# Four edits to a two-block ConvNeXt-style kernel: who asks for x1's rows, when blocks are stored, how many tile reads per place, and how the first pass gives memory back

## The chip, the cores and the metric

The kernel runs on one core of a Trainium2 chip, in one launch. The metric is device time in microseconds, the median of several runs. The engines are TensorE (PE, with its weight loads shown as PEld), VectorE (DVE), ScalarE (ACT), GpSimd (POOL) and SyncE (SP), which only issues DMAs. POOL and ACT can issue DMAs too. Each engine executes its own instructions in order.

## The reference

The input x has shape (8, 96, 96, 192), and all of it is float32. There are two residual blocks, each behind a GroupNorm `gn` with 32 groups. Cut to what matters here:

```python
proj  = einsum('bhwd,dc->bhwc', gn(x), W_in) + b_in          # 192 -> 384 channels
local = depthwise 3x3 convolution of proj
mixed = 0.25 * (four running averages of local: left, right, down, up) + local
x1    = x + layernorm(mixed) @ W_out + b_out                  # 384 -> 192

y = depthwise 7x7 convolution of gn(x1) + dw_bias
y = layernorm(y) * ln_gamma + ln_beta
h = gelu(y @ w0 + b0)                                         # 192 -> 768
out = x1 + (h @ w1 + b1) * gamma                              # 768 -> 192
```

## The kernel before, in words

The work runs in stages. The trace shows them in this order.

The **first pass** (to about 753 us) normalises x, transposes it, multiplies by W_in and writes the projection to a DRAM tensor `P_d`. The last tile is stored by `store_a` (L410 and below), in parts for its channel thirds (`whole(m, eng)`) and one for an edge row.

The **second pass** (770 to 1795 us) loads projection channels (`pin`, issued at L613) and a band of convolution weights (L608), computes the 3x3 convolution as matmuls with banded weights (L626), and does the running averages as scans on DVE (L659, L668) and matmuls. The **third** (to about 2628 us) applies the layer norm and W_out, and writes x1 to DRAM as `X` (`X1_d` in the code).

Then the **7x7 convolution** is done in 32 steps n, one for each half of the batch and each group of channels. A step n loads three raw pieces of x1's rows (`load_raw(n, t)`, t = 0, 1, 2, two DMAs of 384 KB each, L839), loads a band of weights (`load_band`, L849) that DVE copies to the other partitions (`spread`, L877), scales the raw pieces into `xin` (L871 on ACT for the steps in question), runs six convolutions (`conv_d`, 24 matmuls per channel pair, L1196), has ACT write the result into `yo` (L1206), and stores it to DRAM as `Y` with six DMAs on SP (`store_d`, L1222, L1226, L1227).

The **last stage** computes layer norm, both dense layers and the output. It loops over u = 0..72; two values of u share one tile of `Y`, read as two buffers `ya` and `yb`, each in 20 pieces (`load_y`, 60 KB pieces at L1255 and 16 KB pieces at L1261). A tile also needs `r`, the rows of x1 it is added to: `load_r` (L1276, 1536 KB) and `bias_r`, an addition on POOL (L1282). In each u, DVE sums, centres and scales the rows (`norm_steps_e`: L1338, L1331, L1359, and so on), POOL computes the power -1/2 of the variance (L1365), DVE spreads that (L1321 to L1324) and transposes (L1386), PE does the first dense layer (`first_layer`, L1401 and L1411), ACT the gelu (L1420), and PE the second dense layer of the u before (`second_layer`, L1431), after which DVE adds r (L1442) and POOL stores the output (L1450).

The convolutions n = 0..18 run before this loop, and n = 19..31 (`N1` is 19) are laid into it. The order of all of this is written by hand inside `tc.manual_schedule()`. A loop over u calls `slot()` five times; from u = 2 on, each call takes one entry of the list `slots`. A step n has nine entries: three with a third of the scales each, then six with a convolution each. So step n's nine entries spread over nearly two loops u. Besides that, each `slot()` call issues seven steps of the list `loads`, the reads of the next-but-one tile of `Y` (41 steps, begun once per two u).

In the kernel before, the first entry of a step n also asks for its own third raw piece, since only two buffers hold the raw pieces of an inlaid step; the entries after that ask for the first two pieces of n + 1. All are asked for by SP. The last entry, behind the last convolution, asks for the six stores of n and for the band of n + 1. SP's queue in these loops therefore holds the tile's reads ya and yb, r between them, the raw pieces, the stores and the bands, in the order in which the code emits them.

Waits between engines are placed by the framework from the order of emission and from tile lifetimes. Tile pools are opened and closed per stage; a pool opened with `reuse_waits="tile"` lets a later tile on the same memory wait only for the earlier tiles that lay there. Every DMA on the queues of SP and ACT signals its landing on one of eight semaphores, taken in turn, and POOL's DMAs have eight of their own.

Of the kernel before, what the change touches and what calls it, by code (L numbers as in the profile page):

```python
# [101 lines left out]
def conv_blocks_kernel(  # L102
# [40 lines left out]
    L = 2 * S - 1  # L143
    GS = D // GROUPS

    const = ctx.enter_context(tc.tile_pool(name="const", bufs=1))
    dram = ctx.enter_context(tc.tile_pool(name="dram", bufs=1, space=DRAM))

# [2 lines left out]
    RB = 32  # L151
# [50 lines left out]
    SQ = 1.0 - DECAY * DECAY  # L202
    KAPPA = 1.0 / (0.25 * GAIN * SQ)
    ab_pool = ExitStack()
    mp = ab_pool.enter_context(tc.tile_pool(name="ab_const", bufs=1))
    mix = mp.tile([128, NJ, 128], F32, name="mix")
    zero = mp.tile([128, GB, S], F32, name="zero")
    nc.gpsimd.memset(zero, 0.0)
# [27 lines left out]
        (slice(0, 128), 2, slice(DH, D)),  # L236
    )
    with ExitStack() as ph:
        cp = ph.enter_context(tc.tile_pool(name="a_const", bufs=1))
        xp = ph.enter_context(tc.tile_pool(name="a_x", bufs=6))  # L240
        sp = ph.enter_context(tc.tile_pool(name="a_small", bufs=2))
        tp = ph.enter_context(tc.tile_pool(name="a_t", bufs=2))
        op = ph.enter_context(tc.tile_pool(name="a_out", bufs=2))
        zp = ph.enter_context(tc.tile_pool(name="zprep", bufs=1))
        ps_t = ph.enter_context(tc.tile_pool(name="a_ps_t", bufs=2, space=PSUM))
        ps_m = ph.enter_context(tc.tile_pool(name="a_ps_m", bufs=2 * NC, space=PSUM))

        avg = cp.tile([S, 128], F32, name="avg")
        nc.vector.memset(avg, 1.0 / S)
        win = cp.tile([128, 3, C], F32, name="win")  # L250
        for p, k, c in spans:
            nc.scalar.dma_start(win[p, k], W_in[c])
        bin_ = cp.tile([128, NC], F32, name="bin_")
        with nc.allow_non_contiguous_dma(reason="one bias per partition"):
            nc.scalar.dma_start(bin_, b_in.rearrange("(m p) -> p m", p=128))

# [155 lines left out]
        def store_a(po, b, k):  # L412
            at, g = b % GB, b // GB
            final = b == B - 1 and k == NK - 1

            def whole(m, eng):
                eng.dma_start(
                    P_d[
                        g, m * 128 : (m + 1) * 128, k * WA : (k + 1) * WA, at
                    ].rearrange("p r j h -> p r (j h)"),  # L420
                    po[:, m].rearrange("p r j h -> p r (j h)"),
                )

            whole(0, nc.gpsimd)
            if not final:
                for m in range(1, NC):
                    whole(m, nc.gpsimd)

            for edge, r, row, js in (
                (NK - 1, WA - 1, RB, (0, NJ - 1)),  # L430
                (0, 0, RB + 1, (1, NJ)),
            ):
                if k == edge:
                    to = slice(1 - js[0], NJ - js[0])
                    (nc.sync if final else nc.gpsimd).dma_start(
                        P_d[g, :, row, at, to].rearrange("(m p) j h -> p m (j h)", p=128),
                        po[:, :, r, js[0] : js[1]].rearrange("p m j h -> p m (j h)"),
                    )
            if final:
                for m in range(1, NC):  # L440
                    whole(m, (nc.sync, nc.gpsimd)[m % 2])

        def zero_edge(i):

# [53 lines left out]
        with tc.manual_schedule():  # L498
            for n in range(NK):
                for j in range(NJ):  # L500
                    load_a(n, j)
            for n in range(NK, 6):
                for j in range(NJ):
                    load_a(n, j)
            load_kernels()
            bn, last, cols = stats_a(0)
            for step in bn + last:
                step()
            xT = tp.tile([128, 3, WA // 2, S], F32, tag="xT", name="xT")
            for k in range(3):  # L510
                turn(0, cols, xT, k)
            for b in range(B):
                more = b + 1 < B
                for t in range(n_t):
                    u = b * n_t + t

                    n, j = divmod(u - 2, NJ)
                    if j == 0 and n + 6 < n_x:
                        for j in range(NJ):
                            load_a(n + 6, j)  # L520
                    if t == 0 and more:
                        bn, last, nxt_cols = stats_a(b + 1)
                    if u in rest:
                        rest[u]()

                    def ahead(n):
                        if more:
                            for _ in range(n):
                                bn.pop(0)()

                    def end(i):
                        if more:
                            for _ in range(ends.get((t, i), 0)):
                                last.pop(0)()

                    cur = xT
                    if t + 1 < n_t or more:
                        to = cols if t + 1 < n_t else nxt_cols
                        xT = tp.tile([128, 3, WA // 2, S], F32, tag="xT", name="xT")
                        turn_next = lambda k: turn(u + 1, to, xT, k)  # L540
                    else:
                        turn_next = lambda k: None
                    k, j = divmod(t, NJ)
                    if j == 0:
                        po = op.tile([128, NC, WA, NJ, S], F32, tag="po", name="po")
                    pms = project_full(cur)
                    end(0)
                    ahead(share[t] // 2)
                    turn_next(0)
                    turn_next(2)  # L550
                    project_rest(cur, pms, po, j)
                    end(1)
                    ahead(share[t] - share[t] // 2)
                    turn_next(1)
                    if j == NJ - 1:
                        store_a(po, b, k)
                if more:
                    cols = nxt_cols

# [8 lines left out]


    NI = len(place)  # L570
    by_tile = dict(reuse_waits="tile")
    gn_pool = ExitStack()
    gp = gn_pool.enter_context(tc.tile_pool(name="gn", bufs=1, side="right", **by_tile))
    pre = gp.tile([128, 2 * GS, ZW], F32, tag="band", name="c_pre")
# [13 lines left out]
    with ExitStack() as ph:  # L588
# [10 lines left out]
        nc.vector.memset(decay[:, :, 0:1], 0.0)  # L599
        decay_f = decay.rearrange("p b h -> p (b h)")  # L600

        def load_b(k):
            c = slice(k * CC, (k + 1) * CC)
            band = bp_.tile([128, CC, 3, RB], F32, tag="band", name=f"band0_{k}")
            pin = bp_.tile([128, CC, GB, NJ, S], F32, tag="pin", name=f"pin_{k}")
            for g in range(NG):
                p = g * 64
                nc.sync.dma_start(  # L608
                    band[p : p + RB + 4].rearrange("p c t o -> p (c t o)"),
                    ZB_d[:, c].rearrange("r c t o -> r (c t o)"),  # L610
                )
                for lo, hi in ((0, RB), (RB, RB + 1), (RB + 1, RB + 2)):
                    nc.sync.dma_start(  # L613
                        pin[p + lo : p + hi].rearrange("p c b j h -> p c (b j h)"),
                        P_d[g, c, lo:hi].rearrange("c r b j h -> r c (b j h)"),
                    )
            return band, pin

        def conv_b(band, pin, i, last):
            pls = [ps_l.tile([128, GB, S], F32, tag="pl", name="pl") for _ in range(NG)]  # L620
# [69 lines left out]

        n_k = C // CC
        with tc.manual_schedule():
            loads = [load_b(k) for k in range(3)]
            locs, lasts, zs, mos, todo = {}, {}, {}, {}, []

            def add(k, i):
# [115 lines left out]
    s1 = early.tile([128, 2, NH, 2, GROUPS], F32, name="s1")  # L812
    todo = [(hf, i) for hf in range(2) for i in range(NI)]
    N1 = NI + 3
    d_pools = [early, None]
    raws, bands, xins, yos = {}, {}, {}, {}

    def load_raw(n, t):

        hf, i = todo[n]  # L820
        if n >= N1 or ((n == 0 or n % 2) and t < NT - 1):
            pool, bufs = early, NT - 1
        elif n == 0 or n % 2:
            pool, bufs = gp, 1
# [4 lines left out]
        row = NGC * NV * GC * WQ  # L829
        run = NV * GC * WQ  # L830
        x1 = X1_d[hf]
        engs = (nc.sync, nc.gpsimd) if n < 2 else (nc.gpsimd,) * 2 if n < N1 else (nc.sync,) * 2
        for g, eng in enumerate(engs):
            src = bass.AP(
                tensor=x1.tensor,
# [619 lines left out]
    with tc.manual_schedule():  # L1455
# [55 lines left out]
                load_raw(N1, t)  # L1511
        gn_pool.close()
        yp = ctx.enter_context(tc.tile_pool(name="e_yT", bufs=2, side="right", **by_tile))
        rp = ctx.enter_context(tc.tile_pool(name="e_r", bufs=2, side="right", **by_tile))
        tp = ctx.enter_context(tc.tile_pool(name="e_t", bufs=2, side="right", **by_tile))

        slots = []
        for n in range(N1, len(todo)):
            more = n + 1 < len(todo)
            scales = scale_steps(n)  # L1520
            per_t = len(scales) // NT
            slots += [scales[:per_t], scales[per_t : 2 * per_t], scales[2 * per_t :]]
            slots[-3].append(lambda n=n: load_raw(n, NT - 1))
            if more:
                for t in range(NT - 1):
                    slots[t - 2].append(lambda n=n, t=t: load_raw(n + 1, t))
            slots += [[lambda n=n, c=c: conv_d(n, c, ps_y)] for c in range(GS)]
            slots[-1].append(lambda n=n: store_d(n))
            if more:
                slots[-1].append(lambda n=n: load_band(n + 1))  # L1530

        loads = []

        def slot():

            if slots and u >= 2:
                for step in slots.pop(0):
                    step()
            for step in loads[:7]:
                step()  # L1540
            del loads[:7]

        load_r(0, nc.gpsimd)
        for k in range(3):
# [94 lines left out]
```

## Time and profile before

| | |
|---|---|
| median of 3 runs | 5538.36 us (5535.46 to 5547.05) |
| the profiled execution's own time | 5532.09 us |
| its span, first to last instruction | 5530.3 us |
| granted TensorE clock, mean | 0.981 |
| PE busy | 5295.1 us (96%) |
| DVE, ACT, POOL busy | 3600.3, 2587.0, 2317.4 us |

Times in the profile are microseconds from the start of the span. A line of a timeline gives the start, the length, the engine, the line of the kernel, the operation, and the tiles written and read; in square brackets stands how long the engine was idle before it and what ended that. "SPq", "POOLq" and "ACTq" are the DMA requests that an engine's queue makes, with the time that making them took. In lists of waits, the columns are the total, the number of times and the longest, all for a pair of "who waited" and "for what". Matmuls of 32-bit data appear as several records, so counts of matmuls in the profile are larger than in the code.

### The profile page before, as it was taken

The page shows a single profiled execution, that of the slowest core. Times are in us where ns is not written, and L with a number is a line of the kernel's source. Part 1 is how long each engine was busy: PE and PEld are TensorE (multiplying, and loading weights), DVE is VectorE, ACT ScalarE, POOL GpSimd, SP SyncE. Part 2 cuts the span into 40 slices and gives each one's busy share as a digit, 9 for nine tenths or more (in the row PEclk, how much of TensorE's full clock was granted, in tenths as well). Part 3 has the DMA queues.
Part 4 walks back from the last instruction along what each step waited for, and adds up shares of the span by engine and source line. Part 5 has one row for each costly group of instructions (what it writes and reads, how often), then busy time and mean ns, then how long its engine had stood idle before and what let it go on. Part 6 is the DMA issues. An engine that isn't in the chain of part 4 may idle for free. (4 is left out here: it accounts for less than half of the span.)

```text
span 5530.3 us, 108052 instructions
## 1 busy us (share of the span) xinstructions
PE 5295.1 (96%) x42206; PEld 3366.3 (61%) x42206; DVE 3600.3 (65%) x6722; ACT 2587.0 (47%) x5778; POOL 2317.4 (42%) x2021
## 2 busy tenths in 40 slices
PE   6999989999999999999788999999999999999999
PEld 4666643333333899899445555666566667767767
DVE  6656449999999455555556555555467777667764
ACT  2444447777777566565435444444433332332332
POOL 1111128888888455555322222222233333333332
PEclk9999989999999999999899999999999999999999
DMA  7999879999997899899996555555433233333331
GB/s 224 286 289 268 237 195 244 246 241 247 243 245 209 256 291 290 266 286 300 294 281 164 119 121 127 125 134 131 111 91 82 80 80 78 83 94 83 80 79 40
DMA packets 793774, 1015.27 MB, mean 184 GB/s; under 512 B 330623, under 2 KB 669696, under 8 KB 791216
## 3 DMA queue, kind: packets, MB, share of 16 engines
q1 hardware_dynamic: 700104, 673.23, 47.8%
q0 software_dynamic: 82976, 331.44, 18.4%
q8 instruction: 333, 5.46, 0.4%
q10 hardware_dynamic: 10184, 3.70, 0.3%
q14 instruction: 177, 1.45, 0.1%
HBM read 603.70 MB, written 419.95 MB: 185 GB/s over the span
## 5 line engine op out<-in xcount | busy, mean ns | idle before, releaser
L1431 PEld LDWEIGHTS hp<-w1g,g 128*128 128x128 f32 x6912 | 1118.6, 190 | 141.4 <-issue 74.0
L1431 PE MATMUL hp<-w1g,g 128*128 128x192 f32 x6912 | 1175.6, 329 | 0.0
L1420 ACT ACTIVATE g<-hp,b0g 128x512 f32<-128x512 f32 x864 | 518.3, 690 | 1149.9 <-PE hp L1411 1149.8
L1450 POOL DMA_DIRECT2D out_dram<-xo x288 | 210.5, 731 | 1647.9 <-DVE xo L1442 1554.0
L1401 PE MATMUL hp<-yT,w0w 128*128 128x512 f32 x1728 | 781.1, 598 | 10.8 <-DVE yT L1386 10.8
L1442 DVE TENSOR_TENSOR xo<-hp,r 128x384 f32<-128x384 f32 x288 | 227.5, 790 | 816.4 <-PE hp L1431 812.1
L1032 PE MATMUL po<-wc,mt 128*128 128x193 f32 x3456 | 688.0, 335 | 9.1 <-DVE x1c L1049 9.1
L626 PE MATMUL pl<-pin,band 34*32 34x380 f32 (+1 forms) x13824 | 628.7, 490 | 20.4 <-DMA pin<-P_d 20.4
L700 POOL TENSOR_TENSOR mo<-mo,z 128x768 f32<-128x768 f32 x286 | 597.2, 2088 | 4.4 <-ACT mo L651 0.4
L1032 PEld LDWEIGHTS po<-wc,mt 128*128 128x128 f32 x3456 | 557.3, 192 | 40.5 <-ACT mean L1034 30.2
L1196 PE MATMUL hp<-xin,band 63*64 63x372 f32 (+1 forms) x4608 | 433.4, 510 | 126.7 <-ACT yo L1206 39.6
L1401 PEld LDWEIGHTS hp<-yT,w0w 128*128 128x128 f32 x1728 | 322.5, 191 | 373.5 <-issue 337.8
L659 DVE TENSOR_TENSOR_SCAN z<-decay,loc 128x768 f32<-128x768 f32 x288 | 505.8, 1756 | 46.0 <-ACT loc L635 16.5
L668 DVE TENSOR_TENSOR_SCAN z<-decay,z 128x768 f32<-128x768 f32 x288 | 498.3, 1731 | 0.1
L626 PEld LDWEIGHTS pl<-pin,band 34*32 34x32 f32 x13824 | 232.5, 107 | 398.5 <-issue 395.8
L1365 POOL TENSOR_TENSOR rs<-tot,neg_half 32x32 f32<-32x32 f32 x72 | 394.6, 5481 | 105.0 <-DVE tot L1363 104.8
L647 PE MATMUL pa<-loc,mix 128*32 128x384 f32 x3456 | 431.9, 493 | 0.0
L650 PE MATMUL pa<-last,down 96*32 96x384 f32 x1152 | 426.8, 493 | 0.9 <-ACT mo L651 0.9
L1411 PE MATMUL hp<-yT,w0w 64*128 64x512 f32 x1728 | 419.6, 611 | 0.0
L1196 PEld LDWEIGHTS hp<-xin,band 63*64 63x64 f32 x4608 | 225.1, 141 | 304.5 <-issue 168.4
L1206 ACT ACTIVATE yo<-hp,dwb 128x384 f32<-128x384 f32 x384 | 196.2, 582 | 441.1 <-PE hp L1196 289.0
L635 ACT COPY loc<-pl 128x384 f32<-128x384 f32 x576 | 248.2, 483 | 313.0 <-PE pl L626 313.0
(155 smaller groups left out, 7519.1 us busy)
## 6 DMA issues: line engine op xcount, KB each, us to landing
pin<-P_d SPq DMA_DIRECT2D x192, 576.0 KB
P_d<-po POOLq DMA_DIRECT2D x95, 1152.0 KB, 9.7
mt<-M SPq DMA_DIRECT2D x192, 384.0 KB
xq<-in_x_dram SPq DMA_DIRECT2D x96, 576.0 KB
xr<-in_x_dram SPq DMA_DIRECT2D x192, 288.0 KB
X<-x1c SPq DMA_DIRECT2D x144, 384.0 KB
out_dram<-xo POOLq DMA_DIRECT2D x288, 192.0 KB, 2.6
r<-X SPq DMA_DIRECT2D x35, 1536.0 KB
```

The costliest lines, as they stand in the source:

```text
L626: nc.tensor.matmul(pls[g][at * RB : (at + 1) * RB, :, lo:hi], band[rows, c, kh, :], pin[rows, c, :, NJ - 1 - j, lo + kh - 1 : hi + kh - 1] ...
L647: nc.tensor.matmul(pa[at], mix[:, i, at], loc[:, q], start=True, stop=True)
L650: nc.tensor.matmul(pa[at], down[:, to], last[:, q], start=True, stop=True)
L659: nc.vector.tensor_tensor_scan(zf, decay_f, loc.rearrange("p q n -> p (q n)"), 0.0, ALU.mult, ALU.add)
L668: nc.vector.tensor_tensor_scan(zr, decay_f, zr, 0.0, ALU.mult, ALU.add)
L700: eng.tensor_tensor(m, m, z, ALU.add)
L1032: nc.tensor.matmul(po, lhs[m], wc[:, m], start=(m == 0), stop=(m == NC - 1))
L1196: nc.tensor.matmul(pys[g][k * 64 : (k + 1) * 64, :, lo:hi], band[rows, k * GS + c, d * ZS : d * ZS + 64], xin[rows, :, :, k * GS + c, lo + ...
L1401: nc.tensor.matmul(hps[m, q], w0w[:, 0, m * 128 : (m + 1) * 128], yT[:, 2 * q], start=True, stop=False,)
L1411: nc.tensor.matmul(hps[m, q], w0w[p, 1, m * 128 : (m + 1) * 128], yT[p, 1], start=False, stop=True,)
L1420: nc.scalar.activation(g[:, m, q], hps[m, q], AF.Gelu, bias=b0g[:, m : m + 1], scale=1.0)
L1431: nc.tensor.matmul(po[:, q], g[:, m, q, k * 128 : (k + 1) * 128], w1g[:, m], start=(m == 0), stop=(m == NE - 1),)
```

## The change

- **x1's rows.** In the inlaid steps, the raw pieces of n + 1 are asked for by ACT, all three, each right behind the scales of the same third of n. The third piece has a buffer of its own in the pool `e_yT`. The pieces of n = 19 are asked for by POOL, before its first `load_r`.
- **Stores.** The six stores of n and the band of n + 1 move from the last entry of n to the first entry of n + 1, ahead of its scales.
- **Tile reads.** `slot()` issues fourteen steps of `loads` at a call instead of seven, so the 41 steps end after three calls.
- **First pass.** All pools of the first pass give memory back by tile. Of the last tile's stores, the first third is split into halves on POOL and ACT, the edge row goes to ACT, and the other two thirds go to POOL, emitted after the second pass's first loads. The second pass's `pin` tiles get two tags, and the first group's loads of `pin` for k = 0 and 1 are emitted ahead of everything else.

```diff
-            whole(0, nc.gpsimd)
-            if not final:
-                for m in range(1, NC):
+            if final:
+                whole(0, nc.gpsimd, slice(0, 64))
+                whole(0, nc.scalar, slice(64, 128))
+            else:
+                for m in range(NC):
                     whole(m, nc.gpsimd)
...
-                    (nc.sync if final else nc.gpsimd).dma_start(
+                    (nc.scalar if final else nc.gpsimd).dma_start(
...
-            if final:
-                for m in range(1, NC):
-                    whole(m, (nc.sync, nc.gpsimd)[m % 2])
+            return [lambda m=m: whole(m, nc.gpsimd) for m in range(1, NC)]
...
-            loads = [load_b(k) for k in range(3)]
+            tile_b(2)
+            bands_b[0] = tile_band_b(0)
+            for k in range(2):
+                load_pin_b(k, 0)
+            for k in range(3):
+                for g in range(1 if k < 2 else 0, NG):
+                    load_pin_b(k, g)
+                load_band_b(k)
+            loads = [tiles_b[k] for k in range(3)]
+            for step in late_a:
+                step()
...
-        if n >= N1 or ((n == 0 or n % 2) and t < NT - 1):
+        if n >= N1 and t == NT - 1:
+            pool, bufs = d_pools[2], 1
+        elif n >= N1 or ((n == 0 or n % 2) and t < NT - 1):
             pool, bufs = early, NT - 1
...
-        engs = (nc.sync, nc.gpsimd) if n < 2 else (nc.gpsimd,) * 2 if n < N1 else (nc.sync,) * 2
+        engs = (nc.sync, nc.gpsimd) if n < 2 else (eng or nc.gpsimd,) * 2
...
         yp = ctx.enter_context(tc.tile_pool(name="e_yT", bufs=2, side="right", **by_tile))
+        d_pools[2] = yp
+        load_raw(N1, NT - 1)
...
-            slots += [scales[:per_t], scales[per_t : 2 * per_t], scales[2 * per_t :]]
-            slots[-3].append(lambda n=n: load_raw(n, NT - 1))
+            slots += [after + scales[:per_t], scales[per_t : 2 * per_t], scales[2 * per_t :]]
+            after = []
             if more:
-                for t in range(NT - 1):
-                    slots[t - 2].append(lambda n=n, t=t: load_raw(n + 1, t))
+                for t in range(NT):
+                    slots[t - 3].append(lambda n=n, t=t: load_raw(n + 1, t, nc.scalar))
             slots += [[lambda n=n, c=c: conv_d(n, c, ps_y)] for c in range(GS)]
-            slots[-1].append(lambda n=n: store_d(n))
+            after.append(lambda n=n: store_d(n))
             if more:
-                slots[-1].append(lambda n=n: load_band(n + 1))
+                after.append(lambda n=n: load_band(n + 1))
+        slots.append(after)
...
-            for step in loads[:7]:
+            for step in loads[:14]:
                 step()
-            del loads[:7]
+            del loads[:14]
```

## The prediction, made before the result was known

> **What bounds the kernel now.** I read the page first, then busy time by stage, the waits, and timelines round each TensorE (PE) gap.
>
> ```profile
> span 5530.3 us, 108052 instructions
> PE 5295.1 (96%) x42206; PEld 3366.3 (61%) x42206; DVE 3600.3 (65%) x6722; ACT 2587.0 (47%) x5778; POOL 2317.4 (42%) x2021
> ```
>
> PE bounds the span, so only PE's gaps can be won or enlarged. The same by stage (length, then busy PE, PEld, DVE, ACT, POOL, then clock, DMA share, GB/s):
>
> ```profile
> 3025.00:4041.00 1016.00, 965.14 (x5330) 598.70 (x5329) 548.43 (x1023) 460.49 (x804) 276.94 (x146) 0.97 0.53 123
> 4041.00:5525.00 1484.00, 1483.62 (x6718) 1032.29 (x6716) 1001.75 (x1879) 459.04 (x640) 504.14 (x276) 1.00 0.30 79
> ```
>
> With convolutions n=19..31 inlaid (3025 to 4041) PE idles 51 us; without them, 0.4. A row u takes 32.25 us plus 2.2 per inlaid convolution where PE never waits. Against that the thirteen blocks lose, for n=19 on: 10.8, 5.2, 12.8, 2.3, 9.0, 7.3, 0, 1.9, 0, 0, 2.5, 5.0, 13.8: **70.6 us** (gaps, plus some 2 us of slow convolution after each long one: 24 matmuls took 4.04 us behind the 10.16 us gap, 2.55 behind one of 1.78).
>
> ```profile
> POOL r L1282 <- DMA r<-X: 48.1, 5, 13.3
> DVE s L1338 <- DMA yb<-Y: 120.5, 16, 17.7
> ACT xin L871 <- DMA raw<-X: 69.1, 13, 11.5
> PE pl L626 <- DMA pin<-P_d: 20.4, 2, 17.9
> ```
>
> Columns: total, times, longest. Three DMA waits lie behind the gaps (the tile reads yb, the raw rows, and r, which POOL awaits as soon as it can five times); the fourth is the step from the first pass to the second.
>
> **The change part by part.**
>
> *First pass to second: -7 us (-14 to -2).* The last projection result is out at 753.6; PE starts at 770.36 and waits 2.5 us more. SP asked for the second group's pin only at 760.60, its last pieces at 769.42, each behind a whole store's landing. Now only the true halves are waited for; one store is halved between POOL and ACT, the others leave SP. Half of a store's landing (P_d from POOL, 9.7 us on the profile page) is 5 us, and the second gap is 2.5: 7. What follows moves with it: the second pass has 1018 busy in 1019.
>
> *Raw rows of n=19 on POOL: +2 (0 to 5).* Six transfers go ahead of r_0 (2953.96), beside the yb reads for which PE stands 9.07 us at 2978; 2.3 MB more beside them.
>
> *Raw rows in three buffers: -27 (-33 to -12).* 72 requests leave SP. One pair costs it 1.25 us and lands 5.8 us later:
>
> ```profile
> 3202.28 1.25 SPq L839 DMA_DIRECT2D raw<-X  x2
> 3209.33 3.61 ACT L871 ACTIVATE xin<-raw,s 128x192 f32<-128x192 f32 x8 [6.67 <-DMA raw<-X]
> ```
>
> The third scale no longer waits for a late third raw, and yb is in earlier, since SP doesn't sit at a store between its groups. That clears n=20 (5.2), 26 (1.9), 29 (2.5), 30 (5.0), 31 (13.8, of which I keep 1): 27. ACT issues for 72 x 0.62 = 45 us; it is 47% busy and its gelu results are used a row later, so I price this at nothing. If that cover failed, each n would pay up to its six issues, 3.7 us, 45 in all.
>
> *Y reads in fourteens: r goes behind yb.* Forty-one steps now fit into three slots, so r is requested after all forty pieces, not after ya's twenty. Where POOL already waits, that is paid. At n=19:
>
> ```profile
> 3026.09 5.46 POOL L1282 TENSOR_TENSOR r<-r,b1g 128x3072 f32<-128x3072 f32 x1 [13.29 <-DMA r<-X]
> 3031.51 1.45 POOL L1450 DMA_DIRECT2D out_dram<-xo  x2
> 3032.97 5.45 POOL L1365 TENSOR_TENSOR rs<-tot,neg_half 32x32 f32<-32x32 f32 x1
> ```
>
> Behind r's addition stand two output stores and the power that DVE needs (L1321 took it at 3044.20, 5.8 us after its end). There is a second hold. In the records SP's and ACT's DMAs use the same eight landing counters (100, 102 to 108), and each waits for the landing of the DMA that had its counter before. In the changed order yb's 17th and 18th pieces of this tile inherit the counters of ACT's first raw pair, which follows a scale ending at 3034.7: issued by 3036, landed 3041.7. Then the last group (3.9 us), and r is asked for at 3045.5; it lands 7.7 to 8.8 later (3018.45 to 3026.09; 3603.2 to 3612.0), near 3053.8. The power ends at 3053.8 + 5.5 + 1.45 + 5.45 = 3066.2 instead of 3038.4; less the 5.8 of slack, DVE is 22 late. The band copy L877 stands in that chain and PE's convolution waits for it (8.80 us already): **+22** (0 if r came by 3032, up to 30).
>
> Later blocks: r left at 3444.9, 3525.4, 3603.2 and was awaited at once; behind yb it lands near 3472, 3556, 3633, where POOL could use it at 3453, 3534, 3612. Of these 19 to 22 us, 6 to 9 go in POOL's pause before the power, 6 to 7 in DVE's before L1321, some 4 in DVE's idle before xo: 0, 8 and 3 reach PE: **+11** (0 to 20). From the next r on (3675.3) yb no longer meets raws whose landing it must await, and the delay of 10 to 17 us stays inside these pauses.
>
> *Stores a place later, beside ACT's raws.* Store n-1 and band n now stand at the head of n's scales, interleaved with the raws of n+1, and share counters with them. Before, n=22:
>
> ```profile
> 3264.16 0.33 SPq L1222 DMA_DIRECT2D Y<-yo  x1
> 3264.54 0.34 SPq L1226 DMA_DIRECT2D Y<-yo  x1
> 3264.94 2.17 SPq L1227 DMA_DIRECT2D Y<-yo  x1
> 3267.15 2.08 SPq L1222 DMA_DIRECT2D Y<-yo  x1
> 3269.28 0.76 SPq L1226 DMA_DIRECT2D Y<-yo  x1
> 3270.08 3.11 SPq L1227 DMA_DIRECT2D Y<-yo  x1
> 3273.29 1.53 SPq L849 DMA_DIRECT2D band<-Z_d  x1
> ```
>
> ```profile
> 3270.05 3.61 ACT L871 ACTIVATE xin<-raw,s 128x192 f32<-128x192 f32 x8
> 3282.06 3.57 ACT L871 ACTIVATE xin<-raw,s 128x192 f32<-128x192 f32 x8
> ```
>
> After: store two needs raw pair one's landing (3273.7 + 1.2 + 5.8 = 3280.7), store six pair two's (3285.6 + 7.0 = 3292.7). Store six takes 3.1; the band leaves at 3295.8 instead of 3273.3, lands 5.7 later (3192.46 to about 3198.2), and its copy ends at 3303.0, while PE is free at 3291.4: 11.6 + 2 = 13.6 against 2.3. In the same way n=21 (store five behind pair one, 3200): band copy 3211.0 against 3205.1, 7.9 instead of 12.8. n=23 (store six behind r's landing near 3370): 3378.7 against 3365.9, 15 instead of 9. n=24 (band behind pair two, 3443): 3451.2 against 3443.3, 10 instead of 7.3. Together **+15** (-20 to +30: -20 if the bands stay covered and only half of the third raws' wait goes, the whole of it being 31.4; +30 with raws landing 8.4 us after issue, as at 3360.7 to 3369.1). From n=25 on the band leaves within 9 us of before and has that.
>
> *Sum.* -7 + 2 - 27 + 22 + 11 + 15 = **+16** on the profiled execution of 5532.1 (span 5530.3), which is 6.3 under the median of 5538.4: **5554**.
>
> *A rule against the row.* The Trainium skill (DMA: Bandwidth & Descriptors, Issuing engines are not separate DMA queues) says that DMAs from the scalar, sync and gpsimd engines run on the same 16 DMA engines, and that issuing from several saves only the sequencer's time, usually small. By it the move to ACT would gain little, against the 27 above: the sum would be nearer +43, about 5581. The row disagrees in part: DVE stood 12.49 us for yb at 3212.6 with raws between yb's groups in SP's order, so place in the order counts here.
>
> **The rivals.**
> - *r is early enough.* If r came by 3032 in n=19's block and inside the later pauses, 22 + 11 go: -17, 5521, faster. For it: SP drops 72 requests and reaches the tiles sooner. Against: the counter binds the 17th piece to a scale that ended at 3034.7, whatever SP's speed. It decides when n=19's power ends by 3044; at 3049 half of the 22 is lost.
> - *The bands are early enough.* All four go under cover and their 31.4 us vanish: +15 becomes -31, the sum -30, 5508. For it: POOL and SP are less busy, raws might land faster than 5.8. Against: SP's stores, at 9 us per n, are no shorter.
> - *ACT is held.* Every raw it issues waits for the DMA eight places earlier, mostly a yb piece or a store of SP's. If SP is late there, ACT's gelu, scales and yo queue behind it. SP's pieces are mostly 10 to 30 us ahead in my placing, hence nothing; at 3.7 us per n it is +45: 5600.
> - *The memory edit does nothing*, a landing still setting the start: +7, 5561.
>
> **How the numbers follow.** Forecast, both holds real: 0.58, range of its own 5533 to 5580 (0.47 slower, 0.11 same). r early enough: 0.12 (0.07 faster, 0.05 same). Bands early enough: 0.14, faster. ACT held: 0.12, slower. Memory edit without effect: 0.04 (0.01 slower, 0.03 same). So faster 0.21, same 0.19, slower 0.60, with 0.2% (11 us) as about what a measurement can tell from no change. The range 5516 to 5592 leaves out most of the bands' rival and of the held ACT.
>
> **What would show it.** After: PE starts the second pass near 763 to 766 without a second gap. POOL's L1282 ends n=19's r near 3059 (7 earlier by the moved start), and PE stands about 30 us before that convolution. Gaps for bands of 10 us or more before n=22 and 23; none at n=20, 29, 30, 31. L871 hardly waits for raw. Wrong would be: L1196 waiting for ACT's scales or L1401 for gelu (ACT held), or no gap over 10 us at n=19.

## The result, and the profile after

The changed kernel took 5566.67 us (median of 7 runs, 5551.49 to 5575.78) against 5543.82 us for the kernel before (7 runs): ratio **1.0039, 95% interval 1.0021 to 1.0057**. It is slower by about 23 us (12 to 32). The prediction had named 16, slower too.

The line numbers of the changed kernel are about 33 higher in the last stages: L1229 is the inlaid convolution (before: L1196), L904 its scales on ACT, L872 the raw requests, L910 the band copy on DVE, L882 the band's request, L1255 to L1260 the stores, L1309 and L1315 r's request and addition, L1398 the power, L1354 the copy on DVE that takes it up, L1371 the sums of ya and yb, L1386 ACT's squares of them. From the page of the changed kernel:

```profile
span 5574.0 us, 107961 instructions
PE 5311.2 (95%) x42206; PEld 3368.6 (60%) x42206; DVE 3478.2 (62%) x6722; ACT 2584.9 (46%) x5778; POOL 2317.7 (42%) x2028
```

Busy time by stage, of the changed kernel (length, then busy PE, PEld, DVE, ACT, POOL, clock, DMA share, GB/s):

```profile
776.00:1812.00 1036.00, 1035.00 (x18379) 355.66 (x18367) 980.59 (x577) 716.86 (x1726) 871.59 (x945) 0.97 0.89 232
...
3041.00:4086.00 1045.00, 969.15 (x5348) 599.88 (x5347) 535.91 (x1030) 460.72 (x804) 274.87 (x147) 0.96 0.49 120
4086.00:5570.00 1484.00, 1482.10 (x6715) 1031.46 (x6713) 892.77 (x1871) 455.65 (x640) 502.81 (x276) 1.00 0.30 79
```

PE now idles 76 us in the inlaid stretch, 51 before. From the end of row u=0 to that of u=24 (a row ends with its second dense layer) it takes 1040.6 us instead of 1015.8. The tail without convolutions is unchanged at 1484. This profiled execution is 9 us over the median, because its second pass ran at a lower granted clock (1036 us at 0.97, in the execution before 1019 at 0.99, PE busy throughout in both); the last section shows that this isn't the change (one and the same second pass took from 1012 to 1036 us).

Where PE waits, by the changed kernel's list of waits (total, times, longest):

```profile
POOL r L1315 <- DMA r<-X: 233.6, 29, 45.7
DVE band L910 <- DMA band<-Z_d: 87.1, 9, 26.7
PE hp L1229 <- DVE band L910: 51.5, 4, 35.2
DVE s L1371 <- DMA yb<-Y: 44.9, 4, 20.0
DVE m L1354 <- POOL rs L1398: 29.2, 3, 20.3
```

DVE waits less for yb (120.5 us before) and ACT's wait for raw (69.1) has left the list's head, as intended. In their place stand r, the bands, and DVE's wait for the power, which is not among the hundred longest waits of the kernel before. Most of it is one block, n=19. Ahead of it PE stood 8.80 us in the kernel before:

```profile
3055.88 3.99 PE L1196 MATMUL hp<-xin,band 63*64 63x384 f32 x24 [8.80 <-DVE band L877]
```

and 35.21 us in the changed one, by its timeline:

```profile
3040.61 20.21 SPq L1288 DMA_DIRECT2D yb<-Y  x4
...
3053.49 1.28 ACTq L872 DMA_DIRECT2D raw<-X  x2
...
3065.45 0.30 SPq L1294 DMA_DIRECT2D yb<-Y  x1
3065.94 0.38 SPq L1309 DMA_DIRECT2D r<-X  x1
...
3067.44 1.00 DVE L1371 TENSOR_REDUCE s<-yb 128x16 f32<-128x512 f32 x1 [20.01 <-DMA yb<-Y]
...
3077.16 5.41 POOL L1315 TENSOR_TENSOR r<-r,b1g 128x3072 f32<-128x3072 f32 x1 [45.68 <-DMA r<-X]
3082.52 1.45 POOL L1483 DMA_DIRECT2D out_dram<-xo  x2
3083.99 5.45 POOL L1398 TENSOR_TENSOR rs<-tot,neg_half 32x32 f32<-32x32 f32 x1
...
3089.48 0.38 DVE L1354 COPY m<-rs 32x64 f32<-32x64 f32 x2 [20.34 <-POOL rs L1398]
...
3100.97 4.04 PE L1229 MATMUL hp<-xin,band 63*64 63x384 f32 x24 [35.21 <-DVE band L910]
```

Four small requests of SP took 20.21 us. The raw records of the trace say why. They give the start, the length and the number of the landing counter, that is the semaphore on which a DMA's landing is signalled, that was waited for and used:

```
ACT 3053.49 0.61  raw<-X   uses counter 102
ACT 3054.14 0.63  raw<-X   uses counter 104
SP  3058.20 0.30  yb<-Y    idle 17.16 before; waits for 102, uses 102
SP  3060.03 0.30  yb<-Y    idle 1.53 before;  waits for 104, uses 104
```

SP stood 17.16 us for the landing of a raw piece; when it began to wait, ACT had not yet asked for that piece. Then yb's last group, r, r's addition, two output stores and the power follow in a chain, as the prediction had it.

The start of the second pass, in the kernel before and in the changed one:

```profile
770.36 1.45 PE L626 MATMUL pl<-pin,band 34*32 34x384 f32 x2 [17.87 <-DMA pin<-P_d]
...
774.32 5.98 PE L626 MATMUL pl<-pin,band 34*32 34x384 f32 x72 [2.50 <-DMA pin<-P_d]
```

```profile
759.17 5.42 SPq L629 DMA_DIRECT2D pin<-P_d  x3
...
771.26 9.58 PE L647 MATMUL pl<-pin,band 34*32 34x384 f32 x109 [17.41 <-issue]
```

PE stands 17.41 us once, instead of 17.87 and then 2.50.

### The profile page after: what moved, and what is told of

The parts are those of the page before. It is cut to its first block, busy times and chain, and to the rows that moved or that the text cites. A ratio compares the mean times of both kernels' runs of the same rounds, so it can differ in the third digit from the quotient of the medians.

```text
span 5574.0 us, 107961 instructions
## 1 busy us (share of the span) xinstructions
PE 5311.2 (95%) x42206; PEld 3368.6 (60%) x42206; DVE 3478.2 (62%) x6722; ACT 2584.9 (46%) x5778; POOL 2317.7 (42%) x2028
## 5 line engine op out<-in xcount | busy, mean ns | idle before, releaser
L1434 PE MATMUL hp<-yT,w0w 128*128 128x512 f32 x1728 | 782.0, 599 | 18.8 <-DVE yT L1419 17.2
L647 PE MATMUL pl<-pin,band 34*32 34x380 f32 (+1 forms) x13824 | 639.8, 497 | 17.5 <-issue 17.4
L1065 PEld LDWEIGHTS po<-wc,mt 128*128 128x128 f32 x3456 | 554.7, 191 | 39.8 <-ACT mean L1067 30.4
L1229 PE MATMUL hp<-xin,band 63*64 63x372 f32 (+1 forms) x4608 | 431.8, 509 | 149.3 <-DVE band L910 51.5
L1398 POOL TENSOR_TENSOR rs<-tot,neg_half 32x32 f32<-32x32 f32 x72 | 393.4, 5464 | 97.3 <-DVE tot L1396 97.2
L1229 PEld LDWEIGHTS hp<-xin,band 63*64 63x64 f32 x4608 | 224.5, 141 | 326.3 <-issue 174.4
```

The costliest lines, as they stand in the source:

```text
L647: nc.tensor.matmul(pls[g][at * RB : (at + 1) * RB, :, lo:hi], band[rows, c, kh, :], pin[rows, c, :, NJ - 1 - j, lo + kh - 1 : hi + kh - 1] ...
L1065: nc.tensor.matmul(po, lhs[m], wc[:, m], start=(m == 0), stop=(m == NC - 1))
L1229: nc.tensor.matmul(pys[g][k * 64 : (k + 1) * 64, :, lo:hi], band[rows, k * GS + c, d * ZS : d * ZS + 64], xin[rows, :, :, k * GS + c, lo + ...
L1434: nc.tensor.matmul(hps[m, q], w0w[:, 0, m * 128 : (m + 1) * 128], yT[:, 2 * q], start=True, stop=False,)
```

## The experiments

All compare the inlaid loops (end of row u=0 to end of u=24: **1015.8 us before, 1040.6 changed**) and PE's gaps ahead of convolutions, which the clock of the second pass does not touch. Two kernels with the same code in these loops, the kernel before and the one with the first pass's part alone, took 1015.8 and 1016.5. Only the last experiment was timed several times; the others are one execution each.

**Tile reads in sevens.**

```diff
-            for step in loads[:14]:
+            for step in loads[:7]:
                 step()
-            del loads[:14]
+            del loads[:7]
```

> The changed kernel with tile reads in sevens again, all else as changed: r is asked for between ya and yb. Theory (r behind yb feeds POOL's addition and power late): in n=19's block POOL stops waiting 45.7 us for r and DVE no longer waits 20 us for the power; the yb pieces behind ACT's raws still land late (near the time of the changed kernel), so the gap before n=19's convolution falls from 35.2 to about 15 us, and r is awaited by POOL for under 60 us in all instead of 233.6. The gaps at n=22, 23, 24 (5.3, 15.2, 11.0) come from bands and stay within 4 us, but for n=23, where r goes ahead of the stores. Rival (DMA engines carry too much there, order is nothing): the gap at n=19 stays over 30 us.

Inlaid loops 985.0. The gap at n=19 is 18.5 us, and POOL's wait for r fell to 45.2 us: r behind yb counts. But the gaps of n=22 to 24 fell to 0.8, 0 and 0, against what I expected. Sevens move every request after them in the turn of the counters. By the records, the bands of n=22 and 24 now follow requests of SP's own on their counters; that of n=23 still waits 5.0 us for a raw piece of ACT's, but leaves at 3367.87, in time for its convolution at 3378. A new gap of 8.5 came at n=21.

**Stores and band back at the last convolution.**

```diff
-            after.append(lambda n=n: store_d(n))
+            slots[-1].append(lambda n=n: store_d(n))
             if more:
-                after.append(lambda n=n: load_band(n + 1))
+                slots[-1].append(lambda n=n: load_band(n + 1))
```

> The changed kernel with the stores and the band back at the last convolution's place, all else as changed. Theory (stores and bands share landing counters with ACT's raws of the same place and wait for them): the band is asked for before those raws, the gaps at n=22, 23, 24 fall from 5.3, 15.2, 11.0 us to under 3 each, those rows save about 30 us with the slow convolutions behind the gaps; n=19's gap stays at 35. Rival (bands late because SP is busy with yb and r): they fall by less than a third.

Inlaid loops 1015.2. The gaps at n=23 and 24 (15.2, 11.0) are gone, n=19 has 35.6, n=22 keeps 5.2. The row sum fell by 25 instead of 30: the place beside ACT's raws was at fault for two of the three. Small gaps (2.0, 1.5, 1.2, 2.4) came elsewhere.

**Raws on SP, and raws on POOL.** One word each:

```diff
-                    slots[t - 3].append(lambda n=n, t=t: load_raw(n + 1, t, nc.scalar))
+                    slots[t - 3].append(lambda n=n, t=t: load_raw(n + 1, t, nc.sync))
```

> The changed kernel with the raws asked for by SP instead of ACT at the same places. Theory (what delays is that SP waits for the landing of what ACT has yet to ask for): now SP waits in its own queue for the scale that frees the buffer, but not for the landing, so yb's last pieces and the bands leave about 6 us earlier: n=19's gap 35.2 to about 28, n=23's 15.2 to about 9. Rival (ACT's time for the requests is what costs): all gaps at convolutions nearly vanish and ACT's gelu comes 1.3 us earlier per pair.

> The changed kernel with the raws asked for by POOL, whose DMAs have eight landing counters of their own. Theory (shared counters are the hold): SP no longer stops for 20 us inside yb of n=19's block, r is asked for about 20 us earlier there, the gap falls from 35.2 to 8 to 16 us, and the bands of n=22 to 24 come in time: gaps under 4. POOL waits for scales with its output stores behind it, which may cost some us elsewhere. Rival (position and traffic, not counters): n=19 stays over 28 and n=23 over 10.

Raws on SP: 965.4; raws on POOL (`nc.gpsimd`): 965.6. **ACT's queue alone costs 75 us; the rest of the change gains 50.** All gaps but n=19's (10.9 and 12.0) are under 1 us. For SP I had expected much less, and taken by itself this outcome also fits the rival beside my expectation, that ACT's time for asking is what costs. The records speak against that rival: in the changed kernel PE's long gaps wait for bands, and SP stands at counters that ACT's raw pieces hold. And where ACT asks for the same 72 pieces, with sevens or with r on POOL, n=19's gap is not 35.2 us but 18.5 and 15.1. My mistake was to keep SP waiting for the scale inside yb. On its own queue, a raw is asked for after the whole of yb and r, as the code emits it, and in this timeline of the kernel with raws on SP nothing of yb stands behind it:

```profile
3028.13 1.88 SPq L1288 DMA_DIRECT2D yb<-Y  x4
3031.56 0.30 SPq L1294 DMA_DIRECT2D yb<-Y  x1
3032.04 0.38 SPq L1309 DMA_DIRECT2D r<-X  x1
3039.87 10.62 SPq L872 DMA_DIRECT2D raw<-X  x6
```

With two queues that order can be turned round. The eight counters go round one sequence of SP's and ACT's requests together. In the changed kernel's records yb's 11th, 12th and 13th pieces use counters 100, 103 and 105, and ACT's first two raw pieces the two left out, 102 and 104: they have their turn there, ahead of yb's last pieces, although the code emits them later.

**ACT's queue alone, in the kernel before.** Two buffers, stores and sevens as before:

```diff
-        engs = (nc.sync, nc.gpsimd) if n < 2 else (nc.gpsimd,) * 2 if n < N1 else (nc.sync,) * 2
+        engs = (nc.sync, nc.gpsimd) if n < 2 else (nc.gpsimd,) * 2 if n < N1 else (nc.sync,) * 2 if n == N1 and t < NT - 1 else (nc.scalar,) * 2
```

> The kernel before with one part of the change: the raws of the inlaid steps asked for by ACT (two buffers, stores and sevens as before). Theory (SP stops for landings of ACT's requests that come late): the inlaid loops, 1016 us in the kernel before, get longer by 15 to 60 us, with waits of SP inside yb or stores. Rival (a request on another queue is free and relieves SP): shorter, 990 to 1010.

Inlaid loops 1046.2, 30.4 longer. Two of PE's five long waits for a band copy, in its timeline:

```profile
3069.57 4.04 PE L1196 MATMUL hp<-xin,band 63*64 63x384 f32 x24 [23.38 <-DVE band L877]
...
3159.69 4.03 PE L1196 MATMUL hp<-xin,band 63*64 63x384 f32 x22 [12.46 <-DVE band L877]
```

Here, without fourteens, without a third buffer and with the stores at their old place, the one edit makes gaps of 23.4, 12.5, 17.4, 12.8 and 13.1 us. In n=19's block SP again stops inside yb, for 11.4 us until 3038.80, at a counter of ACT's first raw piece (asked for at 3033.91).

**r's request moved to POOL, in the changed kernel.**

```diff
-                load_r(n + 1)
+                load_r(n + 1, nc.gpsimd)
```

> The changed kernel with only r's request moved from SP to POOL, so r stands behind nothing of SP's. It splits n=19's gap of 35.2 us. Theory (20 us of it is the power waiting for r, which waited behind the held yb; the rest is DVE's sum waiting for the held yb itself, which ended at 3068.4): the power is there in time, DVE goes on at once, the gap falls to about 15 us. The gaps of n=22 to 24 (5.3, 15.2, 11.0) have their cause in the bands and stay within 5 us. Rival (r is all of it): under 5.

```profile
3070.39 4.04 PE L1229 MATMUL hp<-xin,band 63*64 63x384 f32 x24 [15.07 <-DVE band L910]
```

15.07 of the 35.2 us remain, as expected: 20 are r's chain, 15 the held yb. n=23 and 24 stay at 14.5 and 9.6; n=22 fell to 0.8, which I had not expected (r out of SP's queue moves the requests behind it in the turn of the counters, and at n=22 the band then follows a store of SP's). n=26's gap fell from 3.6 to 1.0; the next section comes back to it. Inlaid loops 1005.9.

**The same with raws on SP.**

> The changed kernel with the raws asked for by SP and r by POOL, so that r no longer stands behind yb. With the raws on SP alone the one gap left among the inlaid steps was 10.9 us at n=19, behind POOL waiting 21.4 us for r and DVE 11.9 us for the power. Theory (that gap is r behind yb): r lands by about 3030, the power ends before DVE asks for it, the gap falls under 3 us and the inlaid loops u=1 to 24 take 965 - 11 = 954 us. Rival (the yb sums or the band are as late as r): the gap stays over 7.

n=19's gap went from 10.9 to 0.8, the inlaid loops from 965.4 to 956.5. So r behind yb costs 10 us at n=19 where nothing is held, and nothing in later blocks: with raws on SP they have no gap over 1 us, although POOL awaits r 28 times, for 190.7 us.

**Stores back, and sevens, with raws on SP.**

> The changed kernel with the raws on SP and the stores and band back at the last convolution's place. Theory (a place later only hurt because ACT's raws stood beside it; by itself it spares SP the wait for the last result of the convolution): the inlaid loops take 965 to 985 us, with gaps of a few us where DVE waits for yb pieces behind a store. Rival (the place itself is what costs): under 960.

> The changed kernel with the raws on SP and tile reads in sevens. If the fourteens gain by themselves (yb whole before raws and stores come into SP's queue), the inlaid loops grow from 965 to 985 to 1000 us with waits for yb before DVE's sums, as in the kernel before (1016). If r behind yb is the larger effect, they stay at 965 or fall, the gap at n=19 shrinking from 10.9.

Inlaid loops 966.2 and 960.2. With fourteens the stores' place is worth nothing. Sevens are not worse but 5 us better, against the first of the two outcomes I wrote: n=19's gap shrinks to 2.5 and one of 3.8 appears at n=21.

**The third buffer alone, on the kernel before.** `load_raw` as in the change, asked for by SP, sevens, stores and first pass as before:

```diff
-            slots[-3].append(lambda n=n: load_raw(n, NT - 1))
...
-                for t in range(NT - 1):
-                    slots[t - 2].append(lambda n=n, t=t: load_raw(n + 1, t))
+                for t in range(NT):
+                    slots[t - 3].append(lambda n=n, t=t: load_raw(n + 1, t, nc.sync))
```

> The kernel before with one part of the change: a third buffer, so that all three raw pieces of the next step are asked for behind this step's scales; SP asks for them, as before. Theory (the third raw's lateness and SP's stops between yb groups made most of the old gaps): the inlaid loops fall from 1016 to between 955 and 970 us, PE's gaps nearly gone but at n=19. Rival (the gain seen with raws on SP came from the stores' place or the first pass): over 1000.

Inlaid loops 993.9: 22 us gained, not the 46 to 61 I expected. Gaps of 9.9 at n=19, 10.3 at n=21 and 8.4 at n=31 stay. At the last two the band copy stands in DVE's order behind sums that wait 12.6 and 10.7 us for yb, and at n=21 SP asks for that yb's last groups only after six stores, a band and a raw pair. With sevens, the stores a place later bring most of the rest (the last kernel of this section has them too: 971.5).

**The first pass alone, on the kernel before.** Its part of the diff as in the change.

> The kernel before with only the first pass's part of the change. Theory (the start of the second pass is set by the landing of the halved stores and then by the loads behind them): PE idles 17.4 us there instead of 17.9 + 2.5, as in the changed kernel; nothing else moves but the start, 3 us less. Rival (memory given back by tile costs waits in the first pass): the first pass ends later than 753 by more than 3 us.

PE idles 17.35 us at the start of the second pass, with no second gap; the first pass ends at 752.8, the inlaid loops take 1016.5. The part gains 3 us and disturbs nothing.

**The best put together.** All raws on SP, n=19's in their old place with the third behind them; sevens; the rest of the change kept:

```diff
-                load_raw(N1, t)
+                load_raw(N1, t, nc.sync)
...
-        load_raw(N1, NT - 1)
+        load_raw(N1, NT - 1, nc.sync)
```

with the two edits above.

> The changed kernel with all raws of the inlaid steps asked for by SP (n=19's too, in their old place and the third behind them) and tile reads in sevens; first pass, three buffers and the stores' new place stay. Theory (ACT's queue cost 75 us, n=19's raws on POOL some 6 at the start of the last stage, r behind yb some 5): inlaid loops 955 to 962 us, the gap ahead of them back from 15 to 9, the whole 60 to 70 us under the kernel before, ratio 0.987 to 0.989. Rival (chance placement of requests made the former gain): ratio over 0.993.

5485.51 us (6 runs) against 5537.97 (11 runs): **0.9905, interval 0.9884 to 0.9926**, 52 us faster than the kernel before. Less than I expected: the gap ahead of the stage is back at 10.1, but the inlaid loops take 971.5 and not under 962, since n=19's gap is 11.3 us again. With n=19's raws on POOL and all else equal it was 2.5 (the run above with raws on SP and sevens, one execution: 5470.85 us). The two traces show where the difference arises: DVE waits 16.5 us for yb ahead of that gap, 7.0 there. On SP's queue the six raws of n=19 stand ahead of the tile's reads (asked for from 3016.58 on, in 4.2 us), and the twenty pieces of ya behind them take 18.5 us instead of 11.7. The two kernels differ in n=19's raws alone, but each was traced once, and no further run tested it.

## Why the prediction was right, point by point

For the thirteen blocks, row excess in us, by the prediction's own measure (rows without waits taken from the kernel before):

| n | 19 | 20 | 21 | 22 | 23 | 24 | 25 | 26 | 27, 28 | 29 | 30 | 31 | sum |
|---|---|---|---|---|---|---|---|---|---|---|---|---|---|
| before | 10.8 | 5.2 | 12.8 | 2.3 | 9.0 | 7.3 | 0 | 1.9 | 0 | 2.5 | 5.0 | 13.8 | 70.6 |
| predicted | 33 | 0 | 8 | 14 | 15 | 10 | 8 | 3 | 0 | 0 | 0 | 1 | 92 |
| after | 37.8 | 0.2 | 4.8 | 11.2 | 17.2 | 14.2 | 0 | 7.0 | 0 | 1.4 | 0.1 | 1.4 | 95.3 |

- **Raw rows in three buffers, -27.** Measured -23: n=20, 29, 30, 31 are cleared as said. n=26 is not, but for another reason (see r in later blocks). What the experiments add is that the buffer alone gives 22, and only with the stores' place or the fourteens about 50.
- **r behind yb at n=19, +22.** Measured +27. The order of events was the predicted one, to the counter. The 5 us too little lie mostly in r's landing: asked for at 3065.94, it let POOL begin at 3077.16, 11.2 us later, where the prediction had 7.7 to 8.8. Of the gap, 20 us is r's chain and 15 the held yb, by the run with r on POOL. What the prediction blamed first, the place behind yb, is worth 10 us by itself; the hold through the counter makes the rest.
- **r in later blocks, +11.** Measured +5: the 8 us at n=25 did not come, the 3 at n=26 came as 5. Ahead of n=26 DVE waits 7.80 us for the power, which stood behind r's addition (r landed at 3608.88, after POOL had waited 26.07 us). ACT's squares wait for DVE, and the scales come behind the squares:

```profile
3621.36 0.38 DVE L1354 COPY m<-rs 32x64 f32<-32x64 f32 x2 [7.80 <-POOL rs L1398]
...
3630.20 2.05 ACT L1386 ACTIVATE sq<-ya 128x1024 f32<-128x1024 f32 x1 [2.64 <-issue]
...
3653.14 4.46 PE L1229 MATMUL hp<-xin,band 63*64 63x384 f32 x24 [3.57 <-ACT xin L904]
```

With r on POOL, DVE does not wait for that power, ACT's squares wait for nothing, and the gap is 1.02 us, though ACT's first pair of requests took even longer there (3.92 us, against 3.37 in the changed kernel). (Moving r also moves the counters of the requests behind it, so this run changes more than r's place.) The step that failed is the slack at n=25: the prediction took the delay of 19 to 22 us to exceed the pauses of POOL and DVE, and there they absorbed it, for DVE has no wait for that block's power. With raws on SP no block behind n=19 has a gap over 1 us.
- **Stores beside ACT's raws, +15.** Measured +16 (n=21: -8.0, 22: +8.9, 23: +8.2, 24: +6.9). At n=23 the records show what was written: store six waits on counter 108 for r's landing. The band behind it then waits 6.0 us on counter 100, which ACT's third pair had taken at 3402.84, and is asked for at 3414.76.

```profile
3414.76 0.45 SPq L882 DMA_DIRECT2D band<-Z_d  x1
...
3421.14 1.46 DVE L910 COPY band<-band 64x2496 f32<-64x2496 f32 x1 [21.21 <-DMA band<-Z_d]
3422.75 4.04 PE L1229 MATMUL hp<-xin,band 63*64 63x384 f32 x24 [15.22 <-DVE band L910]
```

- **First pass, -7.** Measured -3. The second gap went as said; the first hardly shortened, and that has two reasons in the traces. Halving the store gained little: the whole first store had landed 5.9 us after its request in the kernel before (752.57 to 758.46), not the 9.7 that the prediction took from the profile page, and now POOL's half takes 5.2 and ACT's 7.7 (753.98 to 761.66). The requests at 769.42 are the next channels' already; the second group's last piece left at 766.10. In the changed kernel SP asked for the second group's first piece of `pin` at 759.17 and for the next at 762.52, behind ACT's half and edge row (landed at 762.45). And PE then waits for the first band: its request stands behind these pieces now (764.69), it lands at 771.17, and PE starts at 771.26. In six more runs with this part of the change, too, PE starts 0.1 us behind that landing.
- **n=19's raws on POOL, +2.** Measured +6.7 (15.80 us before the transposes instead of 9.07), above the bound of 5. The nine kernels run with that edit have 14.2 to 19.1 there, the five without it 8.3 to 10.1.
- **ACT's issuing, 0.** It shows once: PE waits 1.52 us at 3321.08 for a gelu that began behind a pair of requests (3318.34, 1.95 us long). That is the sign named for "ACT is held", in one place; PE's waits for scales (2.5 us at n=21, 3.6 at n=26) are no more than single ones of the kernel before.

The sum of the parts that do not hang on the clock is 24.8 + 6.7 - 3.0 = 28.5, the medians say 23 (12 to 32), the prediction said 16. The sign and the mechanism, a shared turn of counters that holds SP, were foreseen. That the sum came so near is in part luck: 6 us too much for r in the later blocks stood against 4 to 5 us too little in each of four terms, the raw rows, r at n=19, the first pass and n=19's raws. The rule weighed there, of the Trainium skill (DMA: Bandwidth & Descriptors, Issuing engines are not separate DMA queues), that more issuing engines save only the sequencer's time, gave an estimate of 5581 in that sum; the measured 5566.67 lies between 5554 and that. But the use made of the rule there was off: in the runs asking from ACT does not merely gain little, it costs 30 us in the one kernel and 75 in the other.

The rivals: "r early enough" failed at n=19, "bands early enough" at n=22 to 24. "ACT is held" came to 1.5 us. "The memory edit does nothing" is nearly true in size (3 us).

## What to carry to other kernels

In a program like this, where two queues share their landing counters, moving DMA requests to the other queue moves them in the shared turn, and a request in front on one queue may then wait for one that another engine makes much later; look in the records at which counters both queues use, and at what stands eight requests ahead. Give the requests that wait for computation the same queue as the prompt ones if they are emitted after them, or a queue with counters of its own. When several edits are made together, take each queue's edit out alone: here one word made a gain of about 50 us into a loss of 25.

## What the runs showed of the hardware that I had not expected

POOL's addition of r holds up a pass of DVE's that starts with it. In the kernel before, DVE's pass over yb (L1331) starts in the same instant as POOL's addition and takes 6.54 us; in the changed kernel, where r comes later, it takes 1.21. The addition takes the same time in both:

```profile
4093.13 6.54 DVE L1331 TENSOR_TENSOR yb<-yb,m 128x1024 f32<-128x1024 f32 x1
...
4093.13 5.44 POOL L1282 TENSOR_TENSOR r<-r,b1g 128x3072 f32<-128x3072 f32 x1
```

```profile
4136.61 1.21 DVE L1364 TENSOR_TENSOR yb<-yb,m 128x1024 f32<-128x1024 f32 x1
...
4139.52 5.42 POOL L1315 TENSOR_TENSOR r<-r,b1g 128x3072 f32<-128x3072 f32 x1 [2.94 <-DMA r<-X]
```

In the last stage 22 such passes are held up before, each together with an addition, and one after. That frees 109 us of DVE (1001.75 busy before, 892.77 after) and moves nothing: PE is busy for 1482 of the 1484 us, and the stage's length is the same.

And one piece of code varies by over 20 us with the granted clock. The second pass of the best kernel and of the kernel with raws on SP, which hold the same code there (length, then busy PE first; the clock is third from the end, before the DMA share and GB/s):

```profile
774.00:1810.00 1036.00, 1035.98 (x18348) 356.37 (x18336) 975.51 (x573) 713.49 (x1718) 869.67 (x942) 0.97 0.88 232
```

```profile
774.00:1788.00 1014.00, 1013.81 (x18355) 351.38 (x18343) 975.61 (x573) 712.90 (x1718) 868.97 (x942) 0.99 0.91 237
```

PE is busy throughout in both, so this pass follows the clock; the shortest, in two other runs, took 1012 us. Single runs of this kernel therefore tell nothing under some 25 us, while the inlaid loops repeated within 1 us in the two kernels that have the same code there.
